# Sharing the last 65 keys over four partition quarters in a fused cross-attention, attention and expert kernel

## The chip, the cores and the metric

The kernel runs on one core of a Trainium2 chip. A core has a matrix engine (PE; its weight loads are shown as PEld), a vector engine (DVE), an activation engine (ACT), a general engine (POOL) and a queue that mostly issues transfers (SP). All of them run at once and wait for each other through semaphores. The metric is the device time of one execution in microseconds; lower is better. "Faster", "the same" and "slower" refer to the median of the runs.

## The reference

Eight batches of 64 query rows and 512 features (512 rows in all) pass through three blocks, each added to its input:

```python
x = x + xattn(layernorm(x), ctx, ctx, Wq, bq, Wk, bk, Wv, bv)   # ctx: 8 x 1601 keys x 512
x = x + attn(layernorm(x), ...)                                 # 16 heads of 32
x = x + ffn(layernorm(x), ...)                                  # one expert of 8 for each row

# xattn
qp = q @ Wq + bq;  kp = ctx @ Wk + bk;  vp = ctx @ Wv + bv
logits = (qp @ kp.T) / sqrt(512)
out = softmax(logits) @ vp
```

The change touches only the first block, with its 1601 keys per batch. 1601 is 12 times 128 and 65 more.

## The kernel before

**Algebra.** The keys are never projected. The queries are projected twice instead (`project_q`, `keyed`), giving `qk = (q Wq + bq) Wk^T`, and the scores are `qk` times the raw context. The term of `bk` is one number for each query row, `qb = qp . bk`; it is computed in `biased(p)` and added through the bias operand of the exponential.

**Tiles.** `p` runs over four pairs of batches; a pair has 128 query rows, 64 for each batch `b2`. The context of a pair is loaded as three groups (`g` 0 to 2) of 512 keys for each batch, 1 MB each (`cx_p_g_b2`), and as a tail (`g` 3) of 65 keys, 65 partitions of 2 KB, in one of two pairs of reused buffers (`tails`). `load_group` issues these on SP's queue. Partition `k` of a group holds four keys.

**Turning the keys.** For the scores the 512 features must lie on partitions. DVE turns 32x32 blocks (`turn_group`, L233 for groups and L240 for tails). The features are handled in four quarters `q` of 128, so a pair needs eight blocked tiles `T_p_q_b2`, each written by three group transposes and one tail transpose. Because a transpose within 32x32 blocks keeps the partition quarter, keys stay in the partition quarter `a` in which they were loaded, and the columns of `T` in quarter `a` are the keys of that quarter: 384 from the groups, and from the tail 32, 32, 1 and 0. This is `WIDTH = (416, 416, 385, 384)`. The tile pool of `T` has five buffers, shared with the probabilities `L_p` and with a blank tile.

**Scores.** `scores(p, q, ...)` (L360) multiplies on a quarter of the PE's rows at a time: for each of four blocks `j` of 32 features, for each partition quarter `a` and each batch, a 32-row by 64-column piece of the array gets the stationary `R` and moves `WIDTH[a]` columns. A product in f32 appears as two instructions. A full round is thus eight matmuls side by side, four row groups by two column groups; a quarter `q` has eight rounds, 64 instructions. The stationary `R` is `qk` spread over the row groups: POOL copies (`spread`, `q4`, L332), PE turns (`fill_queries`, `rt`, L349), ACT copies out (`R`, L352).

**Softmax and values.** `softmax` takes the maxima of the four score banks on DVE (`mx`, L371), then `m`, `nb`, `bias`, then ACT does the exponentials (L382, and L387 for the one key of quarter 2 that is over), each with its sum. `chances` turns the probabilities `L` on PE (`pp`, L404) and ACT copies them out (`pt`, L406). `attend` multiplies them with the context (`ac`, L416); the tail's product contracts 65 rows.

**Order.** PE's order is written out by hand. In pair 0 it is: project the queries, fill `R`, the scores of four quarters, then `keyed(k)` and `biased(k)` for k = 1 to 3, a small product `gs`, `pp` of group 0, the four `rt` steps of pair 1, `pp` of group 1, and `ac`. `biased(0)` stands earlier, before `project_q(1, 3)`. In pairs 2 and 3 the steps of the second block stand between the quarters. On the other engines a scheduler places the instructions when the program is built, from priorities and its own estimates; SP's queue is in such an order too. Each engine then works strictly in its order. The built program gives SP's transfers eight completion semaphores in turn: each issue waits until the transfer eight before it (counting two small ones of ACT) has landed.

## Time and profile before

| what | value |
|---|---|
| median of 3 runs | 298.19 us (298.16 to 298.4) |
| the profiled execution: its own time | 297.94 us |
| its span, first to last instruction | 296.2 us |
| busy in the span: PE, DVE, ACT, POOL | 284.2, 159.0, 92.1, 64.0 us |
| granted PE clock | 0.997 |

The time outside the span of the profiled execution is 1.74 us. A row of the profile such as `L360 PE MATMUL sc<-T,R 32*64 32x416 f32 x512 | 49.5, 513 | 1.8` reads: line, engine, operation, output from inputs, the shape of the array piece and of the operands, the number of instructions, the time in which at least one of them ran, the mean duration of one in ns, and the idle time of the engine just before them with what ended it. Matmuls overlap, so the first number is far below count times mean. In the timeline a row is a start, a duration, the engine, the line and how many instructions were merged.

### The profile page before, as it was taken

What the parts mean: (1) busy time and instruction counts of PE and PEld (TensorE: products, weight loads), DVE (VectorE), ACT (ScalarE), POOL (GpSimd) and SP (SyncE); (2) the same over time, 40 slices, a digit from 0 to 9 for tenths busy, and PEclk for the clock granted to TensorE, in tenths of its full rate; (3) what the DMA queues carried; (4) which work ended last, traced back from release to release, by engine and by line L of the source; (5) the groups of instructions that cost most, each with busy time, mean ns of one, the idle gap of its engine ahead of it and who ended that gap; (6) DMA issues with size and microseconds to landing.
All of it is one profiled execution on the core that took longest, in us unless ns stands there. A gap on an engine that the chain in (4) does not pass through costs nothing. (4 is left out here: it accounts for less than half of the span.)

```text
span 296.2 us, 6460 instructions
## 1 busy us (share of the span) xinstructions
PE 284.2 (96%) x2652; PEld 145.4 (49%) x2652; DVE 159.0 (54%) x412; ACT 92.1 (31%) x202; POOL 64.0 (22%) x109
## 2 busy tenths in 40 slices
PE   6999899999999999999999999999999999999992
PEld 4866655653654334655634465544455456353320
DVE  2464477226654377856668795463272457364140
ACT  2222304340019121236814143651515534120110
POOL 4065200600071101600211310032050032412302
PEclk9999999999999999999999999999999999999998
DMA  6999970179986895000199300959991200523501
GB/s 186 350 408 397 340 318 1 19 284 358 424 292 226 289 385 214 6 3 0 24 387 379 135 2 10 358 198 318 383 375 67 73 0 2 173 74 113 175 3 42
DMA packets 20288, 57.71 MB, mean 195 GB/s; under 512 B 2274, under 2 KB 10514, under 8 KB 16544
## 3 DMA queue, kind: packets, MB, share of 16 engines
q1 hardware_dynamic: 17568, 50.37, 47.5%
q0 software_dynamic: 2400, 6.89, 6.2%
q8 instruction: 23, 0.38, 0.5%
q14 instruction: 9, 0.07, 0.1%
q10 hardware_dynamic: 288, 0.00, 0.1%
HBM read 50.94 MB, written 6.84 MB: 195 GB/s over the span
## 5 line engine op out<-in xcount | busy, mean ns | idle before, releaser
L233 DVE STREAM_TRANSPOSE T<-cx 128x512 f32<-128x512 f32 x96 | 61.8, 680 | 25.2 <-DMA cx<-in_ctx_dram 18.6
L360 PE MATMUL sc<-T,R 32*64 32x416 f32 (+2 forms) x1024 | 49.5, 501 | 1.8 <-DVE T L233 1.2
L416 PE MATMUL ac<-cx,pt 128*64 128x512 f32 x192 | 43.8, 598 | 0.0
L360 PEld LDWEIGHTS sc<-T,R 32*64 32x64 f32 x1024 | 26.6, 131 | 19.3 <-issue 7.1
L416 PEld LDWEIGHTS ac<-cx,pt 128*64 128x64 f32 x192 | 12.7, 136 | 22.4 <-issue 21.6
L981 PE MATMUL gu<-wgu,xeT 128*32 128x512 f32 x192 | 23.0, 597 | 0.0
L492 POOL TENSOR_TENSOR gm_k<-qn_k,c_gk 128x512 f32<-128x512 f32 x4 | 5.1, 1271 | 61.0 <-DVE qn_k L487 61.0
L284 PE MATMUL qp<-xnT,w_xWq 128*128 128x128 f32 (+1 forms) x64 | 16.3, 426 | 0.5 <-ACT xnT L275 0.5
L455 POOL TENSOR_TENSOR x<-x,c_bo 128x512 f32<-128x512 f32 x4 | 5.1, 1270 | 54.3 <-DVE xh L454 54.3
L332 POOL COPY q<-qk 128x512 f32<-128x512 f32 x16 | 9.0, 612 | 34.5 <-ACT qb L324 21.4
L185 PE MATMUL p_qk<-w_xWkT,qpT 128*128 128x512 f32 x32 | 14.9, 605 | 0.0
L185 PE MATMUL p_q<-w_aWq,xhT 128*128 128x512 f32 x32 | 14.8, 605 | 0.0
L185 PE MATMUL p_k<-w_aWk,xhT 128*128 128x512 f32 x32 | 14.7, 595 | 0.0
L185 PE MATMUL p_po<-w_xWv,acT 128*128 128x512 f32 x32 | 14.7, 595 | 0.0
L406 ACT COPY pt<-pp 128x512 f32<-128x512 f32 (+1 forms) x16 | 8.3, 516 | 20.4 <-PE pp L404 20.2
L185 PE MATMUL p_o<-w_aWo,cT 128*128 128x512 f32 x32 | 14.5, 596 | 0.0
L371 DVE TENSOR_REDUCE mx<-sc 128x1 f32<-128x416 f32 (+2 forms) x16 | 8.1, 567 | 11.9 <-PE sc L360 11.9
L185 PE MATMUL p_v<-w_aWv,xvT 128*128 128x512 f32 x32 | 14.4, 592 | 0.0
L284 PEld LDWEIGHTS qp<-xnT,w_xWq 128*128 128x128 f32 x64 | 11.6, 232 | 5.0 <-ACT xnT L275 0.9
L1016 PE MATMUL y<-wd,hT 128*32 128x512 f32 x96 | 11.5, 596 | 0.6 <-DVE hT L1008 0.6
L981 PEld LDWEIGHTS gu<-wgu,xeT 128*32 128x32 f32 x192 | 6.0, 109 | 8.9 <-issue 8.2
L185 PEld LDWEIGHTS p_q<-w_aWq,xhT 128*128 128x128 f32 x32 | 5.7, 189 | 9.0 <-issue 5.9
(190 smaller groups left out, 392.1 us busy)
## 6 DMA issues: line engine op xcount, KB each, us to landing
cx<-in_ctx_dram SPq DMA_DIRECT2D x24, 1024.0 KB, 10.0
wgu<-in_wgT_dram SPq DMA_DIRECT2D x8, 512.0 KB, 9.5
wgu<-in_wuT_dram SPq DMA_DIRECT2D x8, 512.0 KB, 10.3
wd<-in_wdT_dram SPq DMA_DIRECT2D x8, 512.0 KB, 8.9
rd<-blank POOLq DMA_DIRECT2D x6, 258.0 KB, 4.8
in<-rd SPq DMA_DIRECT2D x6, 258.0 KB, 4.6
xd<-blank POOLq DMA_DIRECT2D x6, 256.0 KB, 4.6
in<-xd SPq DMA_DIRECT2D x6, 256.0 KB, 7.2
```

What stands on the lines that cost most here:

```text
L185: nc.tensor.matmul(ps, lhsT=srcT[:, dc, :], rhs=w[:, dc, :], start=(dc == 0), stop=(dc == DC - 1),)
L233: nc.vector.transpose(T[:, :, 128 * g : 128 * g + 128].rearrange("p b (c k) -> p b c k", k=32), cxs[p, g][b2][:, :, 128 * q : 128 * q + 12 ...
L284: nc.tensor.matmul(ps[ec][:, : n * P], lhsT=wq[:, dc, ec * P : (ec + 1) * P], rhs=xnT[:, dc, cols], start=(dc == 0), stop=(dc == DC - 1),)
L332: nc.gpsimd.tensor_copy(q4, qk[:, 32 * b0 : 32 * b0 + 128].rearrange("p (b d) -> p b d", d=32).unsqueeze(2).to_broadcast([P, 4, 4, 32]),)
L360: nc.tensor.matmul(sc[a][r : r + S, : WIDTH[a]], lhsT=R[32 * a : 32 * a + 32, b, r : r + S], rhs=Ts[b2][32 * a : 32 * a + 32, j, : WIDTH[a ...
L371: nc.vector.tensor_reduce(mx[:, a : a + 1], sc[a][:, : WIDTH[a]], AX.X, ALU.max)
L406: nc.scalar.copy(pt[:m, :nch, :], tp[:m, :nch, :])
L416: nc.tensor.matmul(ac[r : r + S, :], lhsT=pt[:m, j, r : r + S], rhs=rhs, start=(g == 0 and j == 0), stop=(g == 3),)
L455: nc.gpsimd.tensor_tensor(xs[i], xs[i], bo, ALU.add)
L492: nc.gpsimd.tensor_tensor(heads(gm), heads(qn), gb.unsqueeze(1).to_broadcast([P, H, HD]), ALU.mult)
L981: nc.tensor.matmul(ps[c, :], lhsT=xTs[k][:, dc, c], rhs=ffw[e][0][:, dc, :], start=(dc == 0), stop=(dc == DC - 1),)
L1016: nc.tensor.matmul(y[c, :], lhsT=hT[:, ic, c], rhs=ffw[e][1][:, ic, :], start=(ic == 0), stop=(ic == IC - 1),)
```

## The change

The 65 keys of a tail are loaded as 17, 16, 16 and 16 rows, at the start of each partition quarter. The tail buffers have 128 partitions and are cleared whole, so that what the 17 or 16 rows leave over is zero. The score widths become 401, 400, 400 and 400. The exponentials of the groups and those of the tail are separate: four of 384 columns and four of 17 or 16, into a chunk 12 of `L` that POOL clears; the sum of the tail's probabilities is a reduction on DVE. `chances` and `attend` use 128 rows for the tail instead of 65.

`biased` becomes one step for all four pairs: for each of four chunks of features, four products with `bk` broadcast to 32 stationary columns, one for each pair in its own column group, moving 128 columns. ACT copies the result `qbT`, PE turns it once (`unturned`, after the first quarter of the scores of pair 0), and DVE copies four columns to `qb`. The three `biased(k)` after the scores of pair 0 and the `biased(0)` before `project_q(1, 3)` are gone; the new step stands after `fill_queries(0, ...)`.

```diff
+    REST = (17, 16, 16, 16)
...
-                nc.sync.dma_start(out=c[: SK - 12 * P, :], in_=src[12 * P :, :])
+                k0 = 12 * P
+                for a, n in enumerate(REST):
+                    nc.sync.dma_start(out=c[32 * a : 32 * a + n, :], in_=src[k0 : k0 + n, :])
+                    k0 += n
...
-    WIDTH = (416, 416, 385, 384)
+    WIDTH = tuple(384 + n for n in REST)
...
-                T[:96, :, 384:416],
+                T[:, :, 384:416],
...
-    def biased(p):
-
-        cols = slice(p * P, (p + 1) * P)
-        ps = bank(f"qb{p}")
+    def biased():
+
+        ps = bank("qb")
         for ec in range(DC):
-            nc.tensor.matmul(
-                ps[:, 0:1], lhsT=qpT[:, ec, cols],
-                rhs=bk[:, ec : ec + 1], start=(ec == 0), stop=(ec == DC - 1),
-            )
-        nc.scalar.copy(qb[:, p : p + 1], ps[:, 0:1])
+            for p in range(NT):
+                nc.tensor.matmul(
+                    ps[32 * p : 32 * p + 32, :P],
+                    lhsT=bk[:, ec : ec + 1].to_broadcast([P, 32]),
+                    rhs=qpT[:, ec, p * P : (p + 1) * P],
+                    start=(ec == 0), stop=(ec == DC - 1),
+                )
+        qbT = rowp.tile([P, P], F32, tag="row", name="qbT")
+        nc.scalar.copy(qbT, ps[:, :P])
+        return qbT
+
+    def unturned(qbT):
+        tp = bank4("t_qb")
+        nc.tensor.transpose(tp[:, 0, :], qbT, ident)
+        nc.vector.tensor_copy(qb, tp[:, 0, ::32])
...
         L = blkp.tile([P, 13, P], F32, tag="blk", name=f"L_{p}")
+        nc.gpsimd.memset(L[:, 12, :], 0.0)
...
         for a in range(4):
-            n = WIDTH[a] // 32
             nc.scalar.activation(
-                L[:, :n, 32 * a : 32 * a + 32],
-                sc[a][:, : 32 * n].rearrange("p (c k) -> p c k", k=32),
+                L[:, :12, 32 * a : 32 * a + 32],
+                sc[a][:, :384].rearrange("p (c k) -> p c k", k=32),
                 AF.Exp, bias=bias, scale=scale, accum_out=sm[:, a : a + 1],
             )
-        nc.scalar.activation(
-            L[:, 12, 64:65], sc[2][:, 384:385], AF.Exp, bias=bias, scale=scale,
-            accum_out=sm[:, 4:5],
-        )
+        for a, n in enumerate(REST):
+            nc.scalar.activation(
+                L[:, 12, 32 * a : 32 * a + n], sc[a][:, 384 : 384 + n],
+                AF.Exp, bias=bias, scale=scale,
+            )
+        nc.vector.tensor_reduce(sm[:, 4:5], L[:, 12, :], AX.X, ALU.add)
...
-        biased(0)
...
     fill_queries(0, R, q4s, 1)
+    qbT = biased()
...
             Ts = nTs
+            if p == 0 and q == 0:
+                unturned(qbT)
...
                 keyed(k)
-                biased(k)
```

The order of the built program changes with it in places that the diff does not name. On DVE the transposes of pair 1 (`T_1_0_0` from `cx_1_0_0`, `cx_1_1_0` and the tail, `T_1_0_1` from `cx_1_0_1` and the tail) stand ahead of `mx_0`, where they stood behind `bias_0`; those of `T_1_1_0` and `T_1_1_1` stand between `mx_0`, `m_0`, `nb_0` and `bias_0`. In pair 1 the first `T_2_0_0` transposes stand ahead of `mx_1` and the tail's of `T_2_0_1` before its last reduction; in pair 2 the first `T_3_0` transposes stand ahead of `cg0`. On SP the loads of `wd0` to `wd2` stand ahead of `wgu1`.

More of the change, by code (lines that the diff above doesn't have):

```diff
@@ L197, in perceiver_kernel @@
     tails = [
-        [one.tile([96, D], F32, tag=f"tail{k}{b2}", name=f"tail{k}{b2}") for b2 in range(2)]
+        [one.tile([P, D], F32, tag=f"tail{k}{b2}", name=f"tail{k}{b2}") for b2 in range(2)]
         for k in range(2)
@@ L202, in perceiver_kernel @@
         for b2 in range(2):
-            nc.gpsimd.memset(tails[k][b2][64:96, :], 0.0)
+            nc.gpsimd.memset(tails[k][b2], 0.0)
+    REST = (17, 16, 16, 16)
     def load_group(p, g):
@@ L395, in softmax @@
         return L, r
-    def extent(g):
-        return (4, P) if g < 3 else (1, SK - 12 * P)
     def chances(p, g, L):
-        nch, m = extent(g)
+        nch = 4 if g < 3 else 1
         tp = bank4(f"pp_{p}_{g}")
         for j in range(nch):
-            nc.tensor.transpose(tp[:m, j, :], L[:, 4 * g + j, :m], ident)
+            nc.tensor.transpose(tp[:, j, :], L[:, 4 * g + j, :], ident)
         pt = row4(f"pt_{p}_{g}")
-        nc.scalar.copy(pt[:m, :nch, :], tp[:m, :nch, :])
+        nc.scalar.copy(pt[:, :nch, :], tp[:, :nch, :])
         return pt
@@ L410, in attend @@
         cx = cxs.pop((p, g))
-        nch, m = extent(g)
-        for j in range(nch):
+        for j in range(4 if g < 3 else 1):
             for b2 in range(2):
                 r = b2 * S
-                rhs = cx[b2][:, j, :] if g < 3 else cx[b2][:m, :]
                 nc.tensor.matmul(
-                    ac[r : r + S, :], lhsT=pt[:m, j, r : r + S], rhs=rhs,
+                    ac[r : r + S, :], lhsT=pt[:, j, r : r + S],
+                    rhs=cx[b2][:, j, :] if g < 3 else cx[b2],
                     start=(g == 0 and j == 0), stop=(g == 3),
```

## The prediction

> **What bounds the kernel now.** I read the busy shares first, then the DMA row, the groups by line, the timeline of pair 0, and the queue of SP.

> ```profile
> PE 284.2 (96%) x2652; PEld 145.4 (49%) x2652; DVE 159.0 (54%) x412; ACT 92.1 (31%) x202; POOL 64.0 (22%) x109
> DMA  6999970179986895000199300959991200523501
> ```

> PE bounds nearly all of it, so a microsecond of PE taken out is one gained, unless PE then waits. In the first five slices (7.4 us each) the transfers are full as well: there they are the second bound.

> ```profile
> L360 PE MATMUL sc<-T,R 32*64 32x416 f32 x512 | 49.5, 513 | 1.8 <-DVE T L233 1.2 <-DVE T L240 0.6
> L360 PE MATMUL sc<-T,R 32*64 32x385 f32 x256 | 44.7, 488 | 0.0
> L320 PE MATMUL qb<-c_xbk,qpT 128*128 128x1 f32 x32 | 3.8, 240 | 0.0
> ```

> The means overlap, so I took starts instead: in the trace two 416-wide matmuls of one row group start 349 ns apart, the 385- and 384-wide ones 323 ns, that is 0.839 ns a column. The row groups do not keep step.

> ```profile
> 32.49 1.30 DVE L233 STREAM_TRANSPOSE T<-cx 128x512 f32<-128x512 f32 x2 [1.19 <-DMA cx<-in_ctx_dram]
> 33.26 8.64 PE L360 MATMUL sc<-T,R 32*64 32x416 f32 x192 [1.23 <-DVE T L233]
> ...
> 42.47 3.02 PE L360 MATMUL sc<-T,R 32*64 32x416 f32 x62 [0.57 <-DVE T L240]
> 45.51 2.02 DVE L371 TENSOR_REDUCE mx<-sc 128x1 f32<-128x416 f32 x4 [3.10 <-PE sc L360]
> ...
> 53.27 4.50 POOL L332 COPY q<-qk 128x512 f32<-128x512 f32 x8 [21.44 <-ACT qb L324]
> 53.28 0.95 PE L320 MATMUL qb<-c_xbk,qpT 128*128 128x1 f32 x8
> 54.09 3.68 PE L185 MATMUL p_qk<-w_xWkT,qpT 128*128 128x512 f32 x8
> 58.64 0.64 PE L404 MATMUL pp<-ident,L 128*128 128x128 f32 x4
> 59.11 1.91 PE L349 MATMUL rt<-ident,q 128*128 128x128 f32 x16
> ```

> The start hangs on one landing: `cx_0_2_1` (32.47) is turned at 32.49 and PE goes at 33.26. Quarter 3 waits for DVE (0.57). After the scores PE has work from 45.41 until `ac` at 61.39, beside which the softmax chain runs; no wait is shown there, so its slack must be worked out.

> ```profile
> 7.21 1.48 SPq L215 DMA_DIRECT2D tail<-in_ctx_dram  x2
> 9.01 5.96 SPq L212 DMA_DIRECT2D cx<-in_ctx_dram  x6
> 15.94 2.68 SPq L215 DMA_DIRECT2D tail<-in_ctx_dram  x2
> ```

> Each SP issue starts as the transfer eight before it lands (9.01 follows the last `w_xWq`, 8.99). That ring of eight is what six more issues per pair use up.

> [...]

> **The change part by part.**

> *Widths.* 416 to 401 columns at 0.839 ns is 12.6 ns a round, 8 rounds, 0.10 us a quarter. Quarters 1 and 2 of pairs 0 and 1 lie behind DVE's chain of transposes (36.38 to 42.42, 6.04 us for three quarters, begun when quarter 0 frees its buffers), so they give nothing. Twelve quarters count: -1.2. In pair 0 DVE's new copy of `qb` (0.15) joins that chain: -1.05 in all. Bounds: -1.6 and 0.

> *`biased`.* From one `qb` row to what follows it is 53.28 to 54.09, 0.81, three times: -2.43. The early one and the new one (32 instructions; as 8 rounds of 4 column groups of 128 columns about 0.95, from 16 `rt` of the same width in 1.91; 0.9 to 2) fall into the wait before 33.26 and cost nothing while that landing is later; the fill was done at 31.12.

> *ACT, POOL, `attend`.* Three more exponentials per pair at ACT's spacing of 0.15 for small ones (+0.4 us), a reduction on DVE, POOL's clear of one chunk: beside PE's work except in pair 0, below. The tail's matmuls on 128 rows instead of 65 move the same columns: 593 and 598 ns in the trace, nothing. DVE's tail transposes (0.27) keep their columns, the tail clear (0.52) too.

> *Start of the transfers.* Eight tail issues stand ahead of `cx_0_0_0`. The seventh and eighth wait for `wkT` to land (12.68, 14.62), so `cx_0_0_0` issues near 15 instead of 9.01; a first packet comes about 1.0 us after an issue, so near 16, where the slowest engine began it at 15.88. Ring time is nearly neutral where 16 rows spread; a 17-row piece on one engine is 17 packets of 2 KB at 84 ns, 1.43 us. Four of the 16 engines lag the others by some 2.3 us until 32 us. If the one with 17 rows is not among them, its 2.9 us nearly fit into the slack: -0.8 to +0.3. If it is: +0.8 to +2. I take +0.1.

> *The stall in pair 0.* This is the step that decides. Before, `mx_0` starts as the scores end, and pair 1's transposes follow behind `bias_0`. After, `T_1_0_0` from `cx_1_1_0`, then a tail, `T_1_0_1` and a tail stand ahead of `mx_0`, so the softmax waits for a landing. Call G the time from the landing of `cx_0_2_1` to that of `cx_1_1_0`. Before it is 44.66 - 32.47 = 12.2. After, on the engine of the 17-row pieces, 4 MB at 2.5 us per MB (8 packets of 313 ns) + 2 x 1.43 + 0.5 of other rows is 13.4; packets beside tails took up to twice as long, so up to 15.6; I take 14.2. Four transposes follow (1.62). Scores end 12.95 after that landing, so `mx_0` is d = G + 1.62 - 12.95 = 2.9 late.

> Then, counted from the end of the scores: `bias_0` comes 4.6 after `mx_0` starts (3.2 before; the transposes of `T_1_1` stand between them), the table load and latency 1.35, eight exponentials 3.0, ACT's copy of `qk1` 0.6 behind them, four POOL copies at 0.56, the last `rt` step 0.5: 12.3 + d = 15.2, and `pp_0_1` puts `ac` at 15.8. PE alone would have it at 61.39 - 45.45 - 2.43 = 13.5. The stall is 2.3 = d - 0.65, and nearly all of `biased`'s gain is gone. Bounds: 0 (G up to 12) and 4.

> *Pair 1.* PE already waits at 91.39 (0.28 for `L`). `T_2_0_0` and a tail transpose (0.1 to 0.3) come ahead of `mx_1`, and before its last reduction `T_2_0_1` from a tail whose last piece issues only after `cx_2_0_0` lands (84.56), behind POOL's blank writes; it is wanted near 87.4. 0.1 to 1.9, I take 0.4.

> *Pairs 2 and 3, late loads.* In pair 2 the `T_3_0` data are there long before (tails 116.8), and DVE has about 0.4 us of room: 0. `wd0` to `wd2` ahead of `wgu1` are first used at 222: 0. Some 24 more SP issues of 0.33 us are beside other work.

> Sum: +0.1 - 1.05 - 2.43 + 2.3 + 0.4 = -0.7 us on a profiled 297.94 (span 296.2 and 1.74 around it): 297.2. That execution is 0.25 under the median of 298.19, so **297.5**.

> **The rivals.**

> *The landings cost more than PE saves* (slower). If engine 0 is a late one or packets beside tails stretch as they did (150 ns instead of 84, 450 to 600 instead of 313), then +1.0 at the start, G = 15.3 with a stall of 3.4, and 0.6 in pair 1 make 5.0 against 3.48: +1.5, **299.7**. It decides once the three waits exceed 3.5 us together. For it speaks that the DMA row is at 9 through the first five slices; against it that only a quarter of the engines were late.

> *All of PE's saving shows.* If 17 rows spread over engines after all, or the tails cease to disturb, G falls to 12.2 or less and the stall to 0.2: -0.3 - 3.48 + 0.2 + 0.1 = -3.5, **294.7**. For it: in the ring the bytes are unchanged, and smaller tails may land sooner; against it: the ring of eight and the place of `mx_0`.

> *The change does not do what it says:* if a round took the sum of its row groups' columns (1601 both times), the scores would give nothing, 1.05 lost: 298.5. The 349 beside 323 ns speak against it; it is within the range.

> **How the numbers follow.** Likeliest 0.44, all saving 0.28, slower 0.25, no gain in the scores 0.03. The likeliest one's own range is 296.4 to 298.6 (stall 1.3 to 3.4). A measurement here can tell about 0.2%, 0.6 us, from no change. Below 297.6 are the 0.28 and about 0.26 of the 0.44: 0.54. Within 0.2%: 0.21, and 0.25 slower. The range runs to both rivals, 294.7 to 299.7, with a little beyond at the top for a larger D and below none: 294.7 to 299.8.

> **What would show it.** Starts of one row group 337 ns apart in all quarters of the scores. No `qb` rows after 45 us, and 32 of them before 33. The first `cx` issue near 15. One late update in the semaphore of a 17-row piece and 16 in that of a 16-row one. DVE waiting for `cx_1_1_0` ahead of `mx_0`, that start some 2.9 us after the scores' end, and PE waiting about 2.3 us at `pp` or `rt` of pair 0, released by ACT's `L` or POOL's `q`. A wait near 88 at `T_2_0_1` from the tail. I am wrong if `mx_0` starts with the scores' end (then near 294.7), or if PE's first score moves by over 1 us (then 299 and more).

## The result, and the profile after

The change makes the kernel slower: 302.19 us (301.13 to 303.62, four runs) against 298.29 us of the kernel before in the same runs, a ratio of 1.0118 with a 95% interval of 1.0072 to 1.0164. The profiled execution took 301.31 us, 299.3 of it the span. Forecast was 297.5, with 294.7 to 299.8 as the range. Ratios and their intervals, here and below, come from the runs in the undisturbed state alone and are not the quotient of the medians, which count every run.

The busy shares and the row of the transfers, of the changed kernel:

```profile
PE 281.2 (94%) x2653; PEld 136.3 (46%) x2653; DVE 160.5 (54%) x417; ACT 93.3 (31%) x207; POOL 64.7 (22%) x113
PEclk9999889999999999999999999999999999999999
DMA  6799993078977597000099504739992200433501
```

PE has 3.0 us less work (281.2 against 284.2), as the change intends, and yet the span is 3.1 us longer. The clock that PE was granted falls in two slices, where it was 9 throughout. Groups by shape and the timeline of the start:

```profile
L374 PE MATMUL sc<-T,R 32*64 32x401 f32 x256 | 49.8, 514 | 3.4 <-DVE T L238 3.2 <-DVE T L245 0.2
L374 PE MATMUL sc<-T,R 32*64 32x400 f32 x768 | 48.2, 512 | 0.0
L325 PE MATMUL qb<-qpT,c_xbk 128*32 128x128 f32 x32 | 1.1, 276 | 0.0
```

```profile
6.09 8.59 SPq L219 DMA_DIRECT2D tail<-in_ctx_dram  x8
14.73 3.17 SPq L214 DMA_DIRECT2D cx<-in_ctx_dram  x6
...
33.77 0.85 PE L374 MATMUL sc<-T,R 32*64 32x401 f32 x2 [1.84 <-DVE T L238]
35.23 1.30 DVE L238 STREAM_TRANSPOSE T<-cx 128x512 f32<-128x512 f32 x2 [0.42 <-DMA cx<-in_ctx_dram]
...
35.99 4.39 PE L374 MATMUL sc<-T,R 32*64 32x401 f32 x62 [1.37 <-DVE T L238]
```

The eight tail issues take until 14.7, and the first `cx` issue follows at 14.73 (9.01 before). `cx_0_2_1` is turned at 35.23 (32.49), and PE's first full round starts at 35.99 (33.26). The windows from 12 to 16 us of the kernel before, and then windows of the changed kernel; the last three columns are the granted PE clock, the share of the transfer engines and GB/s:

```profile
12.00:14.00 2.00, 2.00 (x13) 1.49 (x12) 0.40 (x3) 1.61 (x7) 0.00 (x0) 1.00 1.07 252
14.00:16.00 2.00, 2.00 (x5) 0.68 (x4) 1.93 (x7) 0.08 (x1) 0.00 (x0) 1.00 1.01 322
```

```profile
12.00:14.00 2.00, 1.75 (x4) 0.68 (x4) 1.74 (x5) 0.20 (x1) 0.00 (x0) 1.00 0.38 98
14.00:16.00 2.00, 1.72 (x5) 0.82 (x5) 0.70 (x3) 0.00 (x0) 0.00 (x0) 1.00 0.37 79
24.00:26.00 2.00, 2.00 (x8) 1.18 (x7) 0.00 (x0) 0.00 (x0) 0.00 (x0) 1.00 0.94 248
...
36.00:38.00 2.00, 2.00 (x24) 0.88 (x32) 0.53 (x1) 0.00 (x0) 0.00 (x0) 0.50 1.03 338
38.00:40.00 2.00, 2.00 (x46) 0.86 (x30) 0.00 (x0) 0.00 (x0) 0.00 (x0) 0.75 0.99 349
```

From 12 to 16 us the transfers run at 98 and 79 GB/s, where the kernel before had 252 and 322. From 36 on PE runs at half its clock: 24 matmuls in two microseconds instead of 60 (36 to 38 us of the kernel before). Then the rest of pair 0 and pair 1:

```profile
49.58 0.71 DVE L238 STREAM_TRANSPOSE T<-cx 128x512 f32<-128x512 f32 x1 [2.39 <-DMA cx<-in_ctx_dram]
51.19 1.50 DVE L385 TENSOR_REDUCE mx<-sc 128x1 f32<-128x401 f32 x3
61.04 2.33 PE L363 MATMUL rt<-ident,q 128*128 128x128 f32 x16 [0.34 <-POOL q L346]
63.73 3.65 PE L427 MATMUL ac<-cx,pt 128*64 128x512 f32 x16
...
90.30 0.31 DVE L245 STREAM_TRANSPOSE T<-tail 128x128 f32<-128x128 f32 x1 [0.51 <-DMA tail<-in_ctx_dram]
94.21 0.66 PE L417 MATMUL pp<-ident,L 128*128 128x128 f32 x4 [0.99 <-ACT L L396]
```

DVE does wait for `cx_1_1_0` ahead of `mx_0` (2.39 us), which starts 1.7 us after the scores' end (49.52). In pair 1 it waits for a tail ahead of the last `mx_1`, and PE waits 0.99 for `L`.

I compared the starts of the same instructions in the two profiled executions; the differences between successive points give this account, the forecast beside it:

| where | forecast, us | measured, us |
|---|---|---|
| landing of `cx_0_2_1` (32.47 to 35.20) | +0.1 | +2.73 |
| from that landing to the end of pair 0's scores (12.94 to 14.32) | -0.05 | +1.38 |
| from there to `gs` (13.01 to 10.41): `biased` | -2.43 | -2.60 |
| from `gs` to the first `ac` of pair 0: the stall | +2.3 | +0.83 |
| to the first `p_po` of pair 1 | -0.2 | -0.19 |
| to `p_q` of pair 1 | +0.4 | +0.99 |
| pairs 2 and 3 | -0.8 | -0.52 |
| the rest of the span, and outside it (0.3) | 0 | +0.75 |
| sum | -0.7 | +3.37 |

Rows two, five and seven hold the forecast's -1.05 for the widths, split by pairs. The account rests on one execution of each kernel; what makes the 0.75 of the last row was not looked into.

### The profile page after: what moved, and what is told of

Its sections match the earlier page's. It is cut to its first block, busy times and chain, and to the rows that moved or that the text cites. A ratio compares the mean times of both kernels' runs of the same rounds, so it can differ in the third digit from the quotient of the medians.

```text
span 299.3 us, 6513 instructions
## 1 busy us (share of the span) xinstructions
PE 281.2 (94%) x2653; PEld 136.3 (46%) x2653; DVE 160.5 (54%) x417; ACT 93.3 (31%) x207; POOL 64.7 (22%) x113
## 5 line engine op out<-in xcount | busy, mean ns | idle before, releaser
L374 PE MATMUL sc<-T,R 32*64 32x400 f32 (+1 forms) x1024 | 50.3, 513 | 3.4 <-DVE T L238 3.2
L374 PEld LDWEIGHTS sc<-T,R 32*64 32x64 f32 x1024 | 22.8, 135 | 25.3 <-issue 19.6
L185 PE MATMUL p_qk<-w_xWkT,qpT 128*128 128x512 f32 x32 | 14.5, 600 | 1.8 <-ACT rs_a L267 1.5
L289 PE MATMUL qp<-xnT,w_xWq 128*128 128x128 f32 (+1 forms) x64 | 14.4, 384 | 1.3 <-ACT xnT L280 1.3
L185 PE MATMUL p_q<-w_aWq,xhT 128*128 128x512 f32 x32 | 14.8, 605 | 0.3 <-DVE xhT L475 0.3
L185 PE MATMUL p_k<-w_aWk,xhT 128*128 128x512 f32 x32 | 14.7, 596 | 0.0
L185 PE MATMUL p_po<-w_xWv,acT 128*128 128x512 f32 x32 | 14.6, 594 | 0.0
L185 PE MATMUL p_o<-w_aWo,cT 128*128 128x512 f32 x32 | 14.5, 596 | 0.0
L185 PE MATMUL p_v<-w_aWv,xvT 128*128 128x512 f32 x32 | 14.4, 592 | 0.0
L289 PEld LDWEIGHTS qp<-xnT,w_xWq 128*128 128x128 f32 x64 | 9.6, 191 | 5.7 <-ACT xnT L280 1.8
L385 DVE TENSOR_REDUCE mx<-sc 128x1 f32<-128x400 f32 (+1 forms) x16 | 8.1, 559 | 5.6 <-PE sc L374 5.6
L185 PEld LDWEIGHTS p_qk<-w_xWkT,qpT 128*128 128x128 f32 x32 | 5.8, 190 | 9.6 <-issue 7.9
```

What stands on the lines that cost most here:

```text
L185: nc.tensor.matmul(ps, lhsT=srcT[:, dc, :], rhs=w[:, dc, :], start=(dc == 0), stop=(dc == DC - 1),)
L289: nc.tensor.matmul(ps[ec][:, : n * P], lhsT=wq[:, dc, ec * P : (ec + 1) * P], rhs=xnT[:, dc, cols], start=(dc == 0), stop=(dc == DC - 1),)
L374: nc.tensor.matmul(sc[a][r : r + S, : WIDTH[a]], lhsT=R[32 * a : 32 * a + 32, b, r : r + S], rhs=Ts[b2][32 * a : 32 * a + 32, j, : WIDTH[a ...
L385: nc.vector.tensor_reduce(mx[:, a : a + 1], sc[a][:, : WIDTH[a]], AX.X, ALU.max)
```

## The experiments

Theories after the result. **A**: six more issues fill the ring of eight, so `cx_0_0_0` comes late, the transfer engines run dry, and the long wait of PE halves its clock. **B**: the order on DVE and `biased` make the loss. **C**: the 17-row piece on one engine does. Landing means the last semaphore update of `cx_0_2_1`. All ratios are against the kernel before, on the same chip.

### Splitting the loads alone

```diff
 # kernel before
-                nc.sync.dma_start(out=c[: SK - 12 * P, :], in_=src[12 * P :, :])
+                k0 = 0
+                for n in (17, 16, 16, 16):
+                    nc.sync.dma_start(out=c[k0 : k0 + n, :], in_=src[12 * P + k0 : 12 * P + k0 + n, :])
+                    k0 += n
```

> The kernel before with one edit: each 65-row tail is loaded by four transfers of 17, 16, 16 and 16 rows into the same 65 partitions; nothing else changes. Theory A (the ring of eight is used up by six more issues, so the queue runs dry): the first cx issue moves from 9.0 to 14-15 us, the transfer engines are nearly empty from 12.5 to 15.5, cx_0_2_1 lands at 34.5 to 35.5 instead of 32.5, PE waits about 4 us, the granted clock falls under 0.8 in 36 to 38, and the total rises by 3 to 5 us, to 301.5-303. Theory B (the order of DVE in softmax and the new biased made the loss): within 0.6 us of 298.2.

Measured: 303.02 us, ratio 1.0149 (1.0074 to 1.0223). First `cx` issue 14.33, landing 34.87. Its windows:

```profile
12.00:14.00 2.00, 2.00 (x13) 1.48 (x12) 0.22 (x2) 1.62 (x7) 0.00 (x0) 1.00 0.29 69
14.00:16.00 2.00, 2.00 (x6) 0.85 (x5) 1.93 (x7) 0.07 (x1) 0.00 (x0) 1.00 0.55 98
...
36.00:38.00 2.00, 2.00 (x32) 0.99 (x24) 0.20 (x1) 0.00 (x0) 0.00 (x0) 0.50 1.07 306
```

One edit to the kernel before, which changes no arithmetic, brings the whole picture: the gap, the late landing, the half clock. Splitting the loads is enough for the loss, without anything of B. Whether by the ring (A) or by the 17-row piece (C), this run does not tell, for it holds both; e4_no17 below does.

### The change without the split loads

```diff
 # changed kernel
-                for a, n in enumerate(REST):
-                    nc.sync.dma_start(out=c[32 * a : 32 * a + n, :], in_=src[k0 : k0 + n, :])
-                    k0 += n
+                nc.sync.dma_start(out=c[: SK - 12 * P, :], in_=src[12 * P :, :])
```

> The changed kernel with one transfer of 65 rows per tail as before (partitions 0 to 64, so the keys of the tail stand in the wrong quarters and some are left out of the scores; the amount of work is the same). Theory A: cx_0_2_1 lands near 32.5, no clock below 0.95 after it, and the change keeps PE's savings: 2.4 from biased, about 0.8 from the widths, so 294.5 to 296. Theory B: mx_0 still starts late behind the transposes of pair 1 and the total stays above 298.

Measured: 295.57 us, ratio 0.9902 (0.9874 to 0.9930). First `cx` issue 8.78, DVE turns the landing at 32.27, clock 1.00. `mx_0` still stands behind the transposes of pair 1, but `cx_1_1_0` is there before the scores end, so it starts 1.1 us after them and the timeline shows no wait of PE at `rt`. B falls as the main cause: everything of it is here, and the gain shows.

### biased alone

```diff
 # kernel before, with the changed kernel's biased() and unturned()
-        biased(0)
+    qbT = biased()
...
+            if p == 0 and q == 0:
+                unturned(qbT)
...
-                biased(k)
```

> The kernel before with the new biased alone (widths, tails and transfers as before). Three steps of 0.81 us go from PE behind the scores of pair 0; the order of DVE there is as before. Theory: the softmax chain has slack, so 298.2 - 2.4 + 0.15 (the copy of qb in DVE's chain) = 295.9, between 295.6 and 296.6. Rival: the chain behind mx_0 becomes the bound and half is lost: 297 or more.

Measured: 295.10 us, ratio 0.9874 (0.9795 to 0.9953), a little more than expected. The timeline of PE around the removed steps:

```profile
45.13 10.57 PE L185 MATMUL p_qk<-w_xWkT,qpT 128*128 128x512 f32 x24
...
55.54 0.30 PE L669 MATMUL gs<-c_gwT,ones 128*128 128x32 f32 x2
```

From the scores' end to `gs` are 10.41 us, as in the changed kernel; it was 13.01. The landing came 0.35 earlier in this execution, so the remainder of the gain is not `biased`'s. This part of the change is worth nearly all that the change can be worth.

### The 17-row pieces

```diff
 # changed kernel: sixteen rows in every piece
-                    nc.sync.dma_start(out=c[32 * a : 32 * a + n, :], in_=src[k0 : k0 + n, :])
+                    nc.sync.dma_start(out=c[32 * a : 32 * a + 16, :], in_=src[k0 : k0 + 16, :])
```

> The changed kernel with every tail piece 16 rows long, eight pieces as before at the same places; the last key of each batch is left out. Separates the two causes that the runs so far leave: the ring of eight, full of small issues, and the 17-row pieces on one engine. If the ring alone matters, the first cx issue stays at 13.5 to 14.7, the transfers are thin from 12.5 to 15.5, cx_0_2_1 lands at 34 to 35 and the total is 300-302. If the one engine matters as well in this order, the landing moves by over 1 us, to under 34, and the total to 298-300.

Measured: 302.36 us, ratio 1.0103 (1.0070 to 1.0137); issue 14.36, landing 35.08. (The key that is left out is the 17th of each tail.) In this order the 17th row costs nothing that shows: 35.08 against 35.20. C falls as the cause here. The same trace shows what a longer wait in pair 1 does. PE waits 3.38 us at `pp` for `L`, behind a tail that lands at 91.42, and then its clock is down:

```profile
94.00:96.00 2.00, 0.55 (x5) 0.55 (x6) 0.00 (x0) 2.00 (x11) 0.00 (x0) 1.00 0.29 99
96.00:98.00 2.00, 2.00 (x16) 1.67 (x15) 1.74 (x5) 1.99 (x5) 0.00 (x0) 0.67 0.00 0
```

Pair 1 lost 4.8 us in that execution and 1.0 in the changed kernel's.

### Weaving the tails between the groups

```diff
 # changed kernel, pair 0: cx000, two pieces, cx001, two pieces, ... cx020, cx021
...
+                cxs[p, g].append(load_big(p, g, b2))
+                if g < 2:
+                    load_rest(p, g, (2 * b2, 2 * b2 + 1))
...
```

> The changed kernel with the tails of pair 0 woven between the cx groups on SP: cx000, two pieces, cx001, two pieces, cx010, two pieces, cx011, two pieces, cx020, cx021; DVE takes the tails' transposes later in step. The 17-row pieces remain, and there are still eight pieces. Theory A: first cx issue near 9, no gap in the transfers, cx_0_2_1 lands at 32 to 33.5, no clock drop, total 295.5 to 297.5 (pair 0's late mx_0 and pair 1's wait remain). Theory C (the 17 rows on one engine are what delays all that follows in its ring): cx_0_2_1 lands at 34.5 or later and the total stays above 300.

Measured: 302.44 us, ratio 1.0119 (1.0088 to 1.0150). The first issue is at 6.99 and the gap is gone, 430 and 383 GB/s from 12 to 16 us, but the landing is at 35.55, while its median engine had landed at 31.38. The expectation of theory A missed: without the gap, C decides.

> The woven order of e2_woven with each 17-row piece cut into 16 rows and 1 row, so ten pieces per pair. If the one-engine piece was what kept e2_woven slow (its last engine ran 4 us behind the median), cx_0_2_1 now lands at 32 to 33.5, last and median landing within 2.5 us, the clock does not drop, and the total is 295-297. If the weaving itself (small packets beside 8 KB ones) delays, the landing stays over 34.5 and the total over 300.

With 16 rows and 1 row in place of 17, the landing is 32.87 and the clock does not fall in the scores, so C is shown for this order. The total is still 305.06 us, ratio 1.0215 (1.0131 to 1.0299); the expectation of 295 to 297 missed. The stall has moved to the data of pair 1, which has ten pieces here as well:

```profile
47.66 0.71 DVE L250 STREAM_TRANSPOSE T<-cx 128x512 f32<-128x512 f32 x1 [4.28 <-DMA cx<-in_ctx_dram]
57.48 0.66 PE L428 MATMUL pp<-ident,L 128*128 128x128 f32 x4 [1.05 <-ACT L L413]
59.11 3.37 PE L374 MATMUL rt<-ident,q 128*128 128x128 f32 x16 [0.98 <-POOL q L357]
```

The scores end at 45.71, `mx_0` waits for `cx_1_1_0` and starts 3.6 us later, and PE waits at `pp` and `rt`: the stall of the prediction. From `gs` to the first `ac` are 7.05 us (2.97 in the kernel before). The two waits are half of that difference; most of the rest is the clock, which is at 0.50 from 59.6 to 63.0 us here. In pair 1 PE waits 3.55 for `L`, and the clock falls again.

### Keeping PE busy in the wait

```diff
 # changed kernel
     qbT = biased()
+    idle_turns(36)
```

> The changed kernel with 36 transposes of the identity on PE (3.5 to 4 us, result unused) behind biased, so that PE is not idle while it waits for the landing. If PE's wait is what halves the granted clock: the landing stays near 35.2, the clock is 1.00 in 36 to 40, quarter 0 of the scores takes 2.7 us instead of 4.4 from the landing on, and the total falls by 1.2 to 2 us, to 300.3-301, with less spread between runs. If the low clock has another reason: no change from the changed kernel's 301 to 303.6.

Measured: 301.16 us (299.71 to 304.10), ratio 1.0092 (1.0066 to 1.0118), just over the expected range and without the narrower spread; the total cannot tell it from the changed kernel. The windows can:

```profile
36.00:38.00 2.00, 2.00 (x49) 1.62 (x57) 0.65 (x2) 0.00 (x0) 0.00 (x0) 1.00 1.05 358
38.00:40.00 2.00, 2.00 (x54) 0.87 (x42) 0.87 (x3) 0.00 (x0) 0.00 (x0) 1.00 0.92 312
```

The clock stays at 1.00, and from the landing (35.32) to the end of the scores are 12.84 us instead of 14.32. So the wait itself had halved the clock, at a price of 1.48 by the end of the scores. Most of it is given back at once: `cx_1_1_0` lands no sooner (49.43), and PE waits 0.40 at `pp` and 0.98 at `rt`. From the landing to the first `ac` are 28.27 us, against 28.53 in the changed kernel, so 0.26 of the 1.48 is left. One wait took the place of another. This profiled execution was the slowest of its twenty (304.10): in pair 1 PE waits 2.56 us at `pp` for `L`, and the clock is at 0.50 from 97.0 to 100.5.

### The order on DVE

```diff
 # changed kernel, shortened; biases[p] is the bias instruction of pair p
         T = block_tile(p, q, b2)
-        for g in range(4):
-            turn_group(T, p, q, b2, g)
+        with tc.issue_after(biases[p - 1].ins):   # pairs 1 to 3
+            for g in range(4):
+                turn_group(T, p, q, b2, g)
```

> The changed kernel with the transposes of the next pair queued on DVE behind bias of this pair, as they stood in the kernel before; transfers, widths and biased unchanged. Theory: the late start and the half clock in quarter 0 remain (landing near 35, first cx issue near 14.7), but mx_0 starts with the scores' end, no wait of PE at rt of pair 0 for POOL's q, none at pp of pair 1 over 0.3, so 0.9 + 0.7 us less in the profiled execution and a narrower spread: 299.5 to 300.8. If DVE's order costs nothing: within 0.5 us of 302.2.

Measured: 300.28 us, ratio 1.0048 (1.0017 to 1.0078). The landing is at 34.99 and the half clock lasts even longer here (0.50 through 36 to 40), yet the span is 298.0. `mx_0` starts at 50.60, 0.07 after the scores, and PE does not wait at `rt` of pair 0 and only 0.19 at `pp` of pair 1 (0.28 in the kernel before). From the end of pair 0's scores to `p_q` of pair 1 are 58.22 us, 1.90 less than in the changed kernel. That is what the order which the scheduler chose cost there, and the 0.83 and 0.99 of the account come to the same. The medians also differ by 1.9 (302.19 to 300.28), but their intervals overlap a little; e9_both_batches and e10_both_order below show the same step with intervals that do not.

### Is it POOL's transfer at 24 us?

```diff
 # changed kernel
-    bv = load_b("xbv", D, row("c_xbv"))
+    bv = row("c_xbv")
+    nc.gpsimd.memset(bv, 0.0)
```

> The changed kernel with POOL's load of c_xbv (256 KB, in flight at 23 to 26 us) replaced by a clear, so the bias of the values is left out. Tells whether that transfer is what thins the cx transfers at 24 to 26 us (197 and 299 GB/s against 415 around) once the engines run in step. If so: over 380 GB/s there, cx_0_2_1 lands at 33.7 to 34.4 instead of 35.2, total 300-301.3. If not: the dip stays, the landing is at 35 to 35.4 and the total as the changed kernel's, 301.3-302.6.

Measured: 303.67 us, ratio 1.0148 (1.0049 to 1.0247), landing 34.73. At 24 to 26 us it has 347 GB/s instead of 248, but a dip moves to 26 to 28 (283). The landing gained 0.5, less than expected, and the total is over the expected range: the half clock lasts until 41.1 us and comes again in pair 1, after a wait of 2.68. What thins the transfers there when they start together is not settled.

### Five issues instead of eight

```diff
 # changed kernel; both: the two batches' tails as rows x 2 x 512
...
+            for a in range(4):
+                nc.sync.dma_start(out=c[32 * a : 32 * a + 16], in_=both[16 * a : 16 * a + 16])
+            nc.sync.dma_start(out=c[16:17], in_=both[64:65])
...
```

> The changed kernel with both batches' tails in one buffer of 128 partitions x 2 x 512, loaded by four transfers of 16 rows x 2 batches and one of 1 row x 2: five issues per pair in place of eight, all the 16-row ones on 16 engines. The result is the whole one. First cx issue near 10, no gap, cx_0_2_1 lands at 32 to 33.3, clock 1.00, total 294.8 to 296.3: faster than both kernels by over 0.6%. If six wide issues are needed to starve the ring but five small ones still delay, the landing is over 34 and the total over 298.

Measured: 297.83 us, ratio 0.9990 (0.9952 to 1.0028). First `cx` issue 11.06 and no empty stretch, but the landing is 33.48, just over the expected bound, and the total misses its range by 1.5. The clock, expected at 1.00, is at 0.50 from 13.8 to 17.2 us in this execution, before the scores.

> e9_both_batches with the same order on DVE as e11_order. Theory: e9's waits of PE at rt of pair 0 (0.65) and pp of pair 1 (0.39) go; the landing of cx_0_2_1 stays at 32.5 to 33.5: 295.3 to 297.0, faster than e9 (297.83) by about 1.2. If order costs nothing: 297.5 or more.

With DVE's order added: 296.22 us, ratio 0.9903 (0.9872 to 0.9934); the wait at `rt` is gone and that at `pp` down to 0.20. The landing is 33.91, later than expected, and the transfers move only 162 GB/s from 12 to 16 us, where the kernel before has 287. In the trace's packets the 2 KB rows take 309 ns there (median of 12.0 to 12.5); in the kernel before 167, and 84 alone.

> e10_both_order with the 16 rows of each tail piece written to every eighth partition (a, a+8, ... a+120) instead of sixteen neighbours; the keys of the tail then stand in the wrong places, the amount of work is the same. [...] 2 KB packets at 12 to 13 us take 150 to 200 ns (309 in e10_both_order, 167 in the kernel before, 84 alone), the transfers at 12 to 16 us reach 230 to 300 GB/s (162 in e10_both_order), cx_0_2_1 lands at 32 to 33.1 (33.9) and the total is 294.6 to 296. If short rows are slow wherever they go: packets, landing and total as in e10_both_order (296.2).

```diff
 # e10_both_order
-                    out=c[32 * a : 32 * a + 16], in_=both[16 * a : 16 * a + 16]
+                    out=c[a::8], in_=both[16 * a : 16 * a + 16]
```

Measured: 300.72 us, ratio 1.0074 (1.0051 to 1.0098). The packets do take 169 ns, but the one-row piece overlapped a row of another piece and waited for it; `cx_0_0_0` was issued at 15.35, the engines were empty (7 GB/s from 14 to 16 us), the landing was 35.62 and the clock fell. An unwanted second showing of theory A. With the row on a free partition:

> e13_spread with the one-row piece on a partition that no other piece writes (4 instead of 16). In e13_spread that piece overlapped another one and so waited for its landing, which held cx_0_0_0 back to 15.35 us and emptied the transfers again. Without that wait: first cx issue near 11, 2 KB packets at 12 to 13 us of 150 to 200 ns (309 in e10_both_order), over 230 GB/s at 12 to 16 us (162), cx_0_2_1 at 32 to 33.1 (33.9), total 294.6 to 296. [...]

Measured: 294.82 us, ratio 0.9883 (0.9850 to 0.9915), first `cx` issue 10.29, landing 32.03, packets 159 ns: about twice the 84 ns undisturbed, where those of e10_both_order took 3.7 times as long. From 12 to 16 us the transfer engines were as busy there (a share of 1.11, 162 GB/s) as here (1.05, 324 GB/s), so the placing of the rows is what differs. What in the placing slows them is not shown.

### The version that keeps both gains

```diff
 # e10_both_order: the sixteen keys of a piece on the even partitions of its quarter
+                    out=c[32 * a : 32 * a + 32 : 2], in_=both[16 * a : 16 * a + 16],
...
+            nc.sync.dma_start(out=c[1:2], in_=both[64:65])
...
+                T[:, :, 384:416].rearrange("p b (s i) -> p b i s", s=2),   # even keys first
...
+                L[:, 12, 32 * a : 32 * a + 32 : 2], sc[a][:, 384:400],
```

> The whole computation again: e10_both_order with the sixteen keys of a piece on the even partitions of its quarter [...], the last key on partition 1; DVE's tail transpose writes the even columns first, so a row group still moves 401 or 400 columns, and five small exponentials take the place of four. [...] 2 KB packets of 150 to 190 ns at 12 to 13 us, over 230 GB/s at 12 to 16, cx_0_2_1 lands at 31.8 to 33, total 294.3 to 295.6, as e14_spread_free and faster than e10_both_order. If even partitions help less than every eighth: landing 33.5 or more and 296 or more.

Measured: 294.55 us, ratio 0.9898 (0.9844 to 0.9951), the whole computation. First the window from 12 to 16 us of e10_both_order, then that of this kernel, then its timeline:

```profile
12.00:16.00 4.00, 2.07 (x5) 0.83 (x6) 1.86 (x7) 0.29 (x1) 0.00 (x0) 1.00 1.11 162
```

```profile
12.00:16.00 4.00, 3.91 (x13) 1.70 (x12) 2.93 (x10) 0.39 (x2) 0.00 (x0) 1.00 1.00 333
```

```profile
10.32 5.02 SPq L219 DMA_DIRECT2D cx<-in_ctx_dram  x6
31.72 1.30 DVE L237 STREAM_TRANSPOSE T<-cx 128x512 f32<-128x512 f32 x2 [1.14 <-DMA cx<-in_ctx_dram]
44.70 2.02 DVE L391 TENSOR_REDUCE mx<-sc 128x1 f32<-128x401 f32 x4 [3.00 <-PE sc L380]
57.93 3.65 PE L438 MATMUL ac<-cx,pt 128*64 128x512 f32 x16
```

Twice the bytes pass in the same window, the landing is 31.69, and the first `ac` starts at 57.93 (61.39 before). It beats both kernels; against e8_biased_only (295.10 in other runs) the difference is within what these runs can tell.

## Why the prediction was wrong

**The failed step is "Start of the transfers".** Its parts were right: the eighth issue waits for `wkT`, the first `cx` issue comes near 15 (14.73), its first packet near 16 (15.8), a 17-row piece uses one engine, which no run had shown when it was forecast (two semaphore updates, the second at 14.32; a 16-row piece has sixteen late ones, 11.94 to 14.54, and the 65 rows of the kernel before have 13). The conclusion from them, +0.1, was wrong; it measured +2.73. Of the 4.07 us between the forecast sum and the measured one, 2.63 lie here; next come the unexplained last row of the account (0.75) and pair 1 (0.59). The prediction set the time of the first packet against the slowest engine's 15.88 and took the rest as unchanged. But the slowest engine had begun in the middle of a running stream. After the gap all sixteen begin together (15.79 to 16.25), the first 8 KB packets take a median of 0.79 us instead of 0.31, and `cx_0_0_0` lands at 19.66 (18.23): 1.4 of the 2.7. The slowest engine hid half of the loss: the median engine had `cx_0_0_0` at 16.69 in the kernel before and at 19.44 here, 2.75 later. The rest comes with the dip at 24 to 26 us (248 GB/s, 404 before), whose cause is open. The lateness of "engine 0", on which the bounds stood, played no part (e4_no17).

**A term was missing: the clock.** A wait of PE was priced at its length. It also costs what follows: PE stood from 31.9 to 36.0 but for two matmuls, and the half clock then cost 1.48 by the end of the scores (e3_warm). Between the start and the last matmuls, every half-clock stretch in the traces is 3.41 us (35.59 to 39.01 in the changed kernel) or twice that. PE need not have stood idle for long ahead of one. In the 3.41 us ahead of each fall it worked between 0.7 and 1.6 us: 0.85 in the changed kernel, 1.40 in e3_warm (with its wait of 2.56), 1.37 in e6_woven_16, with two waits of about 1 us close together. After the waits of 1.23 in the kernel before and 0.99 in pair 1 of the changed kernel the clock stayed at 1.00. In e13_spread PE worked 0.85 us from 32 to 36 us at 1.00, and the clock fell only near 37.2.

In the sum this term did little, and that is luck: the clock's row and the stall's together make 1.38 + 0.83 = 2.21, where -0.05 + 2.3 = 2.25 was forecast, because the scores that ended later took up most of the stall.

**The stall of pair 0 was right in mechanism, too large in this execution.** G was put at 14.2 and measured 14.35 (49.55 - 35.20). But the half clock let the scores end later, so `mx_0` was 1.7 late instead of 2.9. By the prediction's own formula, d - 0.65, that is 1.0; measured 0.83. e3_warm shows it without the half clock in the scores: there `mx_0` is 2.90 late, and from `gs` to the first `ac` are 5.03 us against 2.97 in the kernel before, a stall of 2.06 for the forecast 2.3. e11_order shows the cause.

**Pair 1** was named with its place and its bounds of 0.1 to 1.9: 0.99 in the profiled execution, but 4.8 in e4_no17, where PE waited 3.38 and the clock fell again. The bounds lacked that term too.

**`biased` and the widths.** `biased` gave 2.60 for a predicted 2.43. The widths gave less than 0.10 a quarter: in pairs 2 and 3 0.52 in place of 0.8. Eight rounds have seven spacings. Of the row group that ends a quarter, six of them fell from 349 to 336 ns, but the first rose from 374 to 387: 0.065 us a quarter, 0.52 in eight. A mean over all columns would have given nothing, so that rival falls.

**The rivals.** The slower one had the right mechanism and the right point of decision: the three transfer waits made 2.73 + 0.83 + 0.99 = 4.55 against 3.5, and the clock's row 1.38 more. It was given 0.25, and the upper end of the range its sizes. "All of PE's saving shows" gave 294.7, near what the kernel does once the loads and the order on DVE are mended (e14_spread_free, 294.82). The closeness says little: that rival let the 17 rows spread over engines or the tails cease to disturb, and e14_spread_free has other loads, with no 17-row piece and other partitions.

## What to carry to other kernels

Count the issues of a queue, not only its bytes: where completion semaphores are reused in turn, a row of small transfers ahead of large ones can empty the transfer engines (98 and 79 GB/s from 12 to 16 us here, 252 and 322 before). Where waits, one or several close together, may leave PE as little work as ahead of the falls here (0.7 to 1.6 us in 3.41), price the half clock that may follow too (1.48 us here), and ask whether a later wait would have taken up that time anyway. After a change of loads, read the built order of the engines that wait for them: here a scheduler put a wait for a landing ahead of the softmax (1.90 us by e11_order).
